# Attention scores as sums of exact float32r halves instead of float32 products

## The chip, the cores and the metric

One core of a Trainium2 chip runs the kernel. The metric is the device time of one execution in microseconds; the median of three runs is given with the lowest and the highest.

## What is computed

The reference is a chain of four blocks on x, 8 sequences of 512 tokens with 256 features, in float32:

```python
x = x + attn_a(layernorm(x))     # 16 heads of 16, softmax over all 512 keys, biases
x = x + ffn(layernorm(x))        # soft decision tree: 255 gates, 256 leaves
x = x + attn_b(layernorm(x))     # 16 heads of 16, rotary q and k, causal softmax
x = x + ffn(layernorm(x))        # the same tree again
# in both attentions, per sequence and head:
scores = q @ k.T / sqrt(16); out = softmax(scores) @ v
```

The change touches only how q, k, the row maxima of the scores and the products q @ k.T are held and computed.

## The kernel before

A "batch" n runs from 0 to 15: n below 8 is attention a on sequence n followed by the tree, n from 8 on is the causal attention b on sequence n - 8 followed by the tree. All x tiles stay on chip. The 16 heads of a batch are four groups g of four heads j. The four heads of a group lie on partitions 32j to 32j+15 of the q and k tiles, so that their products use four different groups of 32 rows of TensorE. Row 32j+16 of k holds ones (L181), and the same row of q receives minus the maximum of each query's scores, so that one product of 17 rows gives scores less maximum.

The scores are computed twice. The first time (`maxima`, L322, tiles mx) with queries on partitions, so that VectorE reduces each row to its maximum (L348; with the mask, L343, in causal batches). When a group's four query blocks are done, `put` (L352) transposes the maxima (lessT), ScalarE negates them into `rows`, and four DMAs (L360) write them to row 32j+16 of q. The second time (`scores`, L364, tiles st) with keys on partitions; ScalarE takes the exponential into pt (L381), in causal batches GpSimd zeroes the diagonal block (L523), and `weigh` (L383) multiplies with v into av (four heads on four column groups; a column of ones in v gives the sum). `divide` (L401) transposes and normalises.

The main loop (L499) has 32 steps a batch: 4 groups, 4 key blocks kt, 2 pairs of heads. In each step it issues two st products, two mx products of the batch's position 12 steps further on (LEAD, L56), the exponentials and reduces of these four tiles, every second step one `weigh`, and then one piece of other work of kind "pe" and one of kind "v" (`Units`, L63). Other work is written as generators: `pre(n)` (L260: layer norm, transpose, q, k, v), `post` (L425: output projection) and `tree` (L438). `pre(n+1)` is started 12 steps before the first st product of batch n (L509). Causal products are cut to the keys needed: widths of 512, 384, 256 and 128 columns.

PSUM has seven rotating banks (L161) that all these tiles share in order of allocation, and one for av. Each st or mx tile takes one bank until ScalarE or VectorE has read it. Engines run their instructions in order; the order on each is fixed when the program is built, where a scheduler may move an instruction that it expects to wait behind others.

`pre` makes q and k in a layout with feature rows in 128 partitions and moves them into place with DMAs on SP's queue. For n below 8 that is two DMAs of 128 KB for each of four projections' halves (L294). For causal n, ScalarE copies the projection to `eo` (L287), GpSimd computes the rotation in six operations (L302 to L306), and 16 DMAs of 64 KB (L310, eight partitions each at the destination) place q and k. q has two buffers, k two (L179), so the next batch's q is written once the batch before the current one is through.

Of the kernel before, what the change touches and what calls it, by code (L numbers as in the profile page):

```python
# [30 lines left out]

F32 = mybir.dt.float32
AF = mybir.ActivationFunctionType
ALU = mybir.AluOpType
AX = mybir.AxisListType
# [2 lines left out]
P = 128  # L41
# [14 lines left out]
LEAD = 12  # L56
# [45 lines left out]
def hybrid_kernel(ctx, tc, x, a_qk, a_v, a_o, a_qk_b, a_v_b, a_o_b, b_q, b_k, b_v, b_o,  # L102
# [24 lines left out]
    def load_x(b):  # L127
# [5 lines left out]
    make_identity(nc, ident)  # L133
    neg_half = const.tile([P, NT], F32, tag="neg_half", name="neg_half")
    nc.gpsimd.memset(neg_half, -0.5)

    load_x(0)
    wa, wb = Consts(), Consts()
    qk = load(a_qk, "a_qk")
    wa.q, wa.k = qk[:, :, :D], qk[:, :, D:]  # L140
    wa.qk_b = load_as_is(a_qk_b, "a_qk_b")
    wa.v = load(a_v, "a_v")
    load_x(1)
    wa.o = load(a_o, "a_o")
    v_b = load_as_is(a_v_b, "a_v_b")
    out_b = load_row(a_o_b, "a_o_b")

# [7 lines left out]

    raws = [
        load(w, n, pool1, tag)
        for w, n, tag in ((f_q, "f_q", "outT"), (f_routers, "f_routers", "th"),
                          (f_values, "f_values", "lp"), (f_out, "f_out", "lpT"))
    ]  # L160
    banks = ctx.enter_context(tc.tile_pool(name="banks", bufs=7, space=PSUM))  # L161
    ps_av = ctx.enter_context(tc.tile_pool(name="ps_av", bufs=1, space=PSUM))
# [1 line left out]
    def bank(shape, name):  # L164
        return banks.tile(shape, F32, tag="ps", name=name)
# [3 lines left out]
    leaf_scale = load_as_is(leaf_scale, "leaf_scale")  # L169
    for b in range(3, B):  # L170
        load_x(b)
    wb.q, wb.k, wb.v, wb.o = (load(a, n) for a, n in ((b_q, "b_q"), (b_k, "b_k"), (b_v, "b_v"), (b_o, "b_o")))
    cos = load(cos, "cos")[:, 0, :]
    sin = load(sin, "sin")[:, 0, :]


    ks, vs, qs, outs, avs, lesses = [], [], {}, {}, {}, {}
    for i in range(2):
        k = pool1.tile([P, NG, S], F32, tag=f"k{i}", name=f"k{i}")  # L179
        v = pool1.tile([P, NT, H, 2 * HD], F32, tag=f"v{i}", name=f"v{i}")  # L180
        nc.gpsimd.memset(k, 1.0)  # L181
        nc.vector.memset(v, 1.0)
        ks.append(k)
        vs.append(v)

    units = Units()
# [61 lines left out]
    def by_tokens(srcT, w, n, tt, name):  # L248
# [8 lines left out]
                )  # L257
        return ps

    def pre(n):  # L260

        causal, b = divmod(n, B)
        w = wb if causal else wa
        got = []
        yield from layer_norm(b, f"n{n}", got)
        xn = got[0]
        xnT = pool2.tile([P, NC, S], F32, tag="xnT", name=f"xnT{n}")
        qs[n] = pool2.tile([P, NG, S], F32, tag="q", name=f"q{n}")
        for c in range(NC):
            yield "pe", 0 if c else 3  # L270
            transposed(xnT, xn, c, f"xt{n}_{c}")
        for which in range(2):

            dst = (qs[n], ks[n % 2])[which]
            wt = (w.q, w.k)[which]
            if causal:
                eo = pool1.tile([P, 2, S], F32, tag="eo", name=f"eo{n}{which}")
            for c in range(NC):
                yield "pe", 0
                ps = bank([P, S], f"qk{n}{which}{c}")  # L280
                for k in range(NC):
                    nc.tensor.matmul(  # L282
                        ps, lhsT=wt[:, k, c * P : (c + 1) * P], rhs=xnT[:, k, :],
                        start=k == 0, stop=k == NC - 1,
                    )
                if causal:
                    nc.scalar.copy(eo[:, c, :], ps)  # L287
                    continue
                r = pool2.tile([P, S], F32, tag="qk", name=f"r{n}{which}{c}")
                at = 2 * which + c  # L290
                nc.scalar.activation(r, ps, AF.Identity, bias=w.qk_b[:, at : at + 1])
                for j2 in range(2):
                    j = 2 * c + j2
                    nc.sync.dma_start(dst[32 * j : 32 * j + HD, :, :], r[64 * j2 : 64 * j2 + 64, :])  # L294
            if causal:

                yield "v", 0
                by_cos = pool1.tile([P, 2, S], F32, tag="by_cos", name=f"by_cos{n}{which}")
                by_sin = pool1.tile([P, 2, S], F32, tag="by_sin", name=f"by_sin{n}{which}")
                r = pool1.tile([P, 2, S], F32, tag="rot", name=f"rot{n}{which}")  # L300
                for c in range(2):
                    nc.gpsimd.tensor_tensor(by_cos[:, c, :], eo[:, c, :], cos, ALU.mult)  # L302
                    nc.gpsimd.tensor_tensor(by_sin[:, c, :], eo[:, c, :], sin, ALU.mult)
                    yield "v", 0
                nc.gpsimd.tensor_tensor(r[:, 0, :], by_cos[:, 0, :], by_sin[:, 1, :], ALU.subtract)
                nc.gpsimd.tensor_tensor(r[:, 1, :], by_sin[:, 0, :], by_cos[:, 1, :], ALU.add)  # L306
                for c in range(2):
                    for j in range(NJ):
                        at = 32 * j + 8 * c
                        nc.sync.dma_start(dst[at : at + 8, :, :], r[32 * j : 32 * j + 32, c, :])  # L310
        for tt in range(NT // 2):
            yield "pe", 0
            ps = by_tokens(xnT, w.v, D, tt, f"v{n}{tt}")
            for i in range(2):
                to = vs[n % 2][:, 2 * tt + i, :, 0:HD]
                nc.scalar.copy(to, ps[:, i, :].rearrange("p (h d) -> p h d", h=H))
        if n == 0:
            fold_bias()
        if not causal:
            add_bias(b, out_b)  # L320

    def maxima(n, g, u, pair):  # L322

        causal = n >= B
        qt = 3 - (u + LEAD // 2) % NT
        if (u, pair) == (0, 1):
            lesses[n, g] = pool2.tile([P, NJ, NT], F32, tag="less", name=f"less{n}_{g}")
        less = lesses[n, g]
        width = (qt + 1) * P if causal else S
        got = []  # L330
        for j in (2 * pair, 2 * pair + 1):
            rows = slice(32 * j, 32 * j + HD)
            ps = bank([P, S], f"mx{n}_{g}_{qt}_{j}")
            nc.tensor.matmul(  # L334
                ps[:, :width], lhsT=qs[n][rows, g, qt * P : (qt + 1) * P],
                rhs=ks[n % 2][rows, g, :width], start=True, stop=True,
            )
            got.append((j, ps))
        for j, ps in got:
            at = less[:, j, qt : qt + 1]  # L340
            if causal:
                seen = pool2.tile([P, S], F32, tag="seen", name=f"seen{n}_{g}_{qt}_{j}")
                nc.vector.tensor_tensor_reduce(  # L343
                    out=seen[:, :width], in0=ps[:, :width], in1=mask[:, S - width :], scale=1.0,
                    scalar=LOWEST, op0=ALU.add, op1=ALU.max, accum_out=at,
                )
            else:
                nc.vector.tensor_reduce(at, ps, AX.X, ALU.max)  # L348
        if (u, pair) == (NT - 1, 0):
            units.add(put(n, g, lesses.pop((n, g))), "pe", 1, urgent=True)  # L350

    def put(n, g, less):  # L352

        ps = bank([NJ * NT, P], f"lessT{n}_{g}")
        nc.tensor.transpose(ps, less.rearrange("p j t -> p (j t)"), ident)
        rows = pool2.tile([NJ * NT, P], F32, tag="rows", name=f"rows{n}_{g}")
        nc.scalar.mul(rows, ps, -1.0)
        for j in range(NJ):
            at = 32 * j + HD
            nc.sync.dma_start(qs[n][at : at + 1, g, :], rows[NT * j : NT * (j + 1), :])  # L360
        return
        yield

    def scores(n, g, kt, pair):  # L364

        first = kt * P if n >= B else 0
        got = []
        for j in (2 * pair, 2 * pair + 1):
            ps = bank([P, S], f"st{n}_{g}_{kt}_{j}")
            rows = slice(32 * j, 32 * j + HD + 1)  # L370
            nc.tensor.matmul(  # L371
                ps[:, : S - first], lhsT=ks[n % 2][rows, g, kt * P : (kt + 1) * P],
                rhs=qs[n][rows, g, first:], start=True, stop=True,
            )
            got.append((j, ps))
        return got

    def exponentials(n, kt, got, pt):
        width = S - kt * P if n >= B else S
# [45 lines left out]
    def post(n):  # L425

        causal, b = divmod(n, B)
        outT = pool1.tile([P, NC, S], F32, tag="outT", name=f"outT{n}")
        out = outs.pop(n)
        for c in range(NC):  # L430
            transposed(outT, out, c, f"outTp{n}_{c}")
# [6 lines left out]
    def tree(n, b):  # L438
# [20 lines left out]
        for level in range(DEPTH):  # L459
# [12 lines left out]
                        pairs[:, :, :, side], of_level, one, lp, ALU.add, ALU.mult  # L472
                    )
            lp = new
        lpT = pool1.tile([P, NC, S], F32, tag="lpT", name=f"lpT{n}")
        for c in range(NC):
            yield "pe", 0 if c else 1
            transposed(lpT, lp, c, f"lt{n}_{c}")
# [20 lines left out]
    for i in range(-LEAD, total + 2):  # L499
        ahead = i + LEAD  # L500
        if ahead < total:
            n, g, u, pair = place(ahead, 1)
            if ahead % STEPS == 0:
                if n in pres:
                    units.finish(pres.pop(n))
                if 0 < n < 2 * B - 1:
                    if n + 1 >= B:
                        units.finish(trees[n + 1 - B])
                    pres[n + 1] = units.add(pre(n + 1))  # L509
        got = None  # L510
        if 0 <= i < total:
            sn, sg, kt, sp = place(i, 0)
            if sp == 0:
                pt = pool3.tile([P, NJ, S], F32, tag="pt", name=f"pt{sn}_{sg}_{kt}")
            got = scores(sn, sg, kt, sp)
        if ahead < total:
            maxima(n, g, u, pair)
        if got is not None:
            exponentials(sn, kt, got, pt)
            if sp == 1:  # L520
                if sn >= B:

# [71 lines left out]
```

## Time and profile before

| what | us |
|---|---|
| median of 3 runs (lowest to highest) | 1599.61 (1596.56 to 1602.42) |
| the profiled execution | 1595.46 |
| its span (first to last instruction) | 1593.7 |
| TensorE busy | 1481.2 |
| VectorE busy | 757.5 |
| ScalarE busy | 665.9 |
| GpSimd busy | 453.8 |
| mean granted TensorE clock | 0.862 |

Busy is the time in which at least one instruction of the engine runs. A row of the page's groups gives the line, the engine, the operation, output<-inputs, the shape and count, then the busy time and the mean duration of one in ns, then the idle time before it and what ended it. st and mx products overlap in time, so their busy times may not be added. A float32 product appears as two records, each with its own weight load (engine PEld). First st products of the batches start at 79.96 (n=0), 154.3, 245.1, 342.7, 441.1, 531.5, 633.0, 732.8, 824.1 (n=8, the first causal one), 921.8, 1011.3, 1106.0, 1195.6, 1290.3, 1379.9 and 1470.6. The page's other large groups:

```profile
L381 ACT ACTIVATE pt<-st 128x512 f32<-128x512 f32 (+3 forms) x1024 | 473.7, 517 | 488.1 <-PE mx L334 413.8
L348 DVE TENSOR_REDUCE less<-mx 128x1 f32<-128x512 f32 x512 | 328.5, 684 | 301.0 <-PE mx L334 300.3
L390 PE MATMUL av<-pt,v 128*32 128x512 f32 (+3 forms) x2048 | 272.3, 608 | 27.9 <-POOL pt L523 27.8
```

The exponential and the reduce both spend most of their idle time waiting for TensorE.

### The profile page before, as it was taken

Reading aid. Unit: us, or ns where it says so; the run is one execution under the profiler, and the core shown is the slowest. Engines: PE = TensorE matmul, PEld = TensorE weight load, DVE = VectorE, ACT = ScalarE, POOL = GpSimd, SP = SyncE. Lnnn points to the kernel's source line nnn. Section 1 sums busy time; section 2 is a strip of 40 time slices with the busy share of each in tenths; the row PEclk is TensorE's granted clock in tenths of the full one; section 3 lists DMA queues with packets and bytes.
Section 4 is the critical chain, followed back from the end, with each engine's and each line's share of the span. In section 5 each row is a group of like instructions: output and inputs, shape, how many; then the busy total and the mean of one; then the engine's idle time right before and its main releaser. Section 6 shows DMA issues by size and latency. Waiting matters only on the chain.

```text
span 1593.7 us, 22833 instructions
## 1 busy us (share of the span) xinstructions
PE 1481.2 (93%) x8276; PEld 668.1 (42%) x8276; DVE 757.5 (48%) x2247; ACT 665.9 (42%) x1443; POOL 453.8 (28%) x452
## 2 busy tenths in 40 slices
PE   4999999999999999999998898989889798989895
PEld 2333444334344434433444444445445343445444
DVE  2355655546546555455544343544444344544422
ACT  1155545445445444545454342534334343433331
POOL 7000300402104040032416245451624445251312
PEclk9599999889799988979999596977979787986767
DMA  7001001000010100100101000000101001010000
GB/s 230 17 11 18 11 1 27 2 17 12 2 27 1 28 1 1 28 1 8 22 1 28 1 14 15 23 19 14 28 1 32 10 23 19 15 28 2 14 14 13
DMA packets 24847, 31.09 MB, mean 20 GB/s; under 512 B 4000, under 2 KB 16032, under 8 KB 24736
## 3 DMA queue, kind: packets, MB, share of 16 engines
q1 hardware_dynamic: 24736, 29.64, 7.9%
q8 instruction: 66, 1.08, 0.3%
q14 instruction: 45, 0.37, 0.1%
HBM read 8.13 MB, written 4.19 MB: 8 GB/s over the span
## 4 chain that ended last, share of the span: by engine, by line
PE 84%; POOL 7%; DVE 6%; issue 1%; ACT 1%; DMA 1%; SPq 0%; POOLq 0%; DVEq 0%; ACTq 0%
PE st L371 26%; PE av L390 15%; PE mx L334 10%; PE qk L282 8%; PE z L254 5%; PE ty L254 4%; PE v L254 4%; PE y L254 4%; DVE lp L471 3%; POOL xnt L233 2%; POOL xnn L233 2%; PE oT L407 2%; PE txt L245 2%; PE lt L245 2%; PE outTp L245 1%
## 5 line engine op out<-in xcount | busy, mean ns | idle before, releaser
L381 ACT ACTIVATE pt<-st 128x512 f32<-128x512 f32 (+3 forms) x1024 | 473.7, 517 | 488.1 <-PE mx L334 413.8
L334 PE MATMUL mx<-k,q 16*128 16x512 f32 (+3 forms) x2048 | 623.5, 631 | 6.1 <-issue 6.1
L371 PE MATMUL st<-q,k 17*128 17x512 f32 (+3 forms) x2048 | 565.2, 619 | 33.4 <-DMA q<-rows 29.6
L348 DVE TENSOR_REDUCE less<-mx 128x1 f32<-128x512 f32 x512 | 328.5, 684 | 301.0 <-PE mx L334 300.3
L343 DVE CUSTOM_DVE_ANT_0 seen<-mx,mask 128x512 f32<-128x512 f32 (+3 forms) x512 | 230.7, 487 | 340.5 <-PE mx L334 331.2
L390 PE MATMUL av<-pt,v 128*32 128x512 f32 (+3 forms) x2048 | 272.3, 608 | 27.9 <-POOL pt L523 27.8
L371 PEld LDWEIGHTS st<-q,k 17*128 17x128 f32 x2048 | 183.6, 208 | 232.9 <-issue 152.2
L334 PEld LDWEIGHTS mx<-k,q 16*128 16x128 f32 x2048 | 219.5, 209 | 58.5 <-ACT pt L381 28.5
L523 POOL TENSOR_SCALAR_AFFINE_SELECT pt<-pt 128x512 f32<-128x512 f32 x128 | 81.6, 640 | 431.8 <-ACT pt L381 431.1
L229 POOL TENSOR_SCALAR ln_rstdt<-ln_mvt 128x4 f32<-128x4 f32 x16 | 3.7, 232 | 592.9 <-DVE ln_mvt L225 592.9
L390 PEld LDWEIGHTS av<-pt,v 128*32 128x32 f32 x2048 | 43.0, 115 | 199.8 <-issue 139.5
L254 PE MATMUL z<-wg,txnT 128*128 128x255 f32 x256 | 79.7, 466 | 0.5 <-ACT txnT L246 0.5
L233 POOL TENSOR_SCALAR xnt<-x,ln_mvt,ln_rstdt 128x256 f32<-128x256 f32 x64 | 77.4, 1221 | 0.3
L233 POOL TENSOR_SCALAR xnn<-x,ln_mvn,ln_rstdn 128x256 f32<-128x256 f32 x64 | 77.4, 1220 | 0.1
L254 PE MATMUL ty<-wl,lpT 128*128 128x256 f32 x256 | 73.1, 436 | 0.0
L254 PEld LDWEIGHTS z<-wg,txnT 128*128 128x128 f32 x256 | 57.2, 235 | 35.6 <-issue 10.9
L282 PE MATMUL qk<-xnT,a_qk 128*128 128x512 f32 x128 | 68.0, 661 | 0.0
L254 PEld LDWEIGHTS ty<-wl,lpT 128*128 128x128 f32 x256 | 52.5, 216 | 32.0 <-DVE x L423 8.3
L471 DVE SCALAR_TENSOR_TENSOR lp<-th,lp 128x8 f32<-128x8 f32 (+6 forms) x224 | 64.0, 322 | 3.3
L302 POOL TENSOR_TENSOR by_cos<-eo,cos 128x512 f32<-128x512 f32 x32 | 40.7, 1270 | 80.4 <-ACT eo L287 80.4
L407 PE MATMUL oT<-ident,o 128*128 128x128 f32 x256 | 47.2, 313 | 10.6 <-DVE less L343 7.8
L407 PEld LDWEIGHTS oT<-ident,o 128*128 128x128 f32 x256 | 30.4, 155 | 58.6 <-ACT pt L381 20.9
(74 smaller groups left out, 1143.8 us busy)
## 6 DMA issues: line engine op xcount, KB each, us to landing
x<-x SPq DMA_DIRECT2D x8, 512.0 KB
q<-r SPq DMA_DIRECT2D x32, 128.0 KB
k<-r SPq DMA_DIRECT2D x32, 128.0 KB
q<-rows SPq DMA_DIRECT2D x256, 2.0 KB
q<-rot SPq DMA_DIRECT2D x64, 64.0 KB
k<-rot SPq DMA_DIRECT2D x64, 64.0 KB
out<-x SPq DMA_DIRECT2D x8, 512.0 KB
a_qk<-a_qk SPq DMA_DIRECT2D x1, 512.0 KB
```

Source lines behind the costliest of these rows:

```text
L233: nc.gpsimd.tensor_scalar(xn[:, t, :], x[:, t, :], mv[:, t, 0:1], rstd[:, t : t + 1], ALU.subtract, ALU.mult)
L254: nc.tensor.matmul(ps[:, i, :n], lhsT=srcT[:, c, t * P : (t + 1) * P], rhs=w[:, c, :], start=c == 0, stop=c == NC - 1,)
L282: nc.tensor.matmul(ps, lhsT=wt[:, k, c * P : (c + 1) * P], rhs=xnT[:, k, :], start=k == 0, stop=k == NC - 1,)
L334: nc.tensor.matmul(ps[:, :width], lhsT=qs[n][rows, g, qt * P : (qt + 1) * P], rhs=ks[n % 2][rows, g, :width], start=True, stop=True,)
L343: nc.vector.tensor_tensor_reduce(out=seen[:, :width], in0=ps[:, :width], in1=mask[:, S - width :], scale=1.0, scalar=LOWEST, op0=ALU.add, ...
L348: nc.vector.tensor_reduce(at, ps, AX.X, ALU.max)
L371: nc.tensor.matmul(ps[:, : S - first], lhsT=ks[n % 2][rows, g, kt * P : (kt + 1) * P], rhs=qs[n][rows, g, first:], start=True, stop=True,)
L381: nc.scalar.activation(pt[:, j, :width], ps[:, :width], AF.Exp, scale=SCALE)
L390: nc.tensor.matmul(av[32 * j : 32 * j + 32, first:], lhsT=vs[n % 2][:, kt, g * NJ + j, :], rhs=pt[:, j, : S - first], start=kt == 0, stop= ...
L407: nc.tensor.transpose(ps[:, t, :, :].rearrange("p j d -> p (j d)"), o4[:, t * P : (t + 1) * P], ident)
L471: nc.vector.scalar_tensor_tensor(pairs[:, :, :, side], of_level, one, lp, ALU.add, ALU.mult)
L523: nc.gpsimd.affine_select(out=pt[:, :, :P], in_=pt[:, :, :P], pattern=[[0, NJ], [1, P]], compare_op=ALU.is_ge, fill=0.0, base=0, channel_m ...
```

## The change

float32r is a 32-bit format with fewer mantissa bits; a tile of that type holds rounded values. q and k are each kept as hi, the rounded value, and lo, the rest (`halves`). k holds hi on rows 32j to 32j+15 and lo on the next 16; q is kept twice, once as hi and lo and once as lo and hi. Two passes over 32 rows, one with each q tile, then add up hi*hi + lo*lo + lo*hi + hi*lo. The negated maxima are kept as two halves too, in tiles m of their own (two rows per head), and a third pass with a stationary tile of ones adds them to st. `products` replaces the products of `maxima` and `scores`: it takes the banks of all four products of a step and issues first pass by first pass, then the second passes, then the third.

```diff
+    def halves(raw, which, n, at, js, height):
+        hl = pool2.tile([P, 2, S], F32R, tag="hl", name=f"hl{n}{which}{at}")
+        nc.scalar.copy(hl[:, 0, :], raw)
+        lo_on = nc.vector if n >= B else nc.gpsimd
+        lo_on.tensor_tensor(hl[:, 1, :], raw, hl[:, 0, :].bitcast(F32), ALU.subtract)
+        hl = hl.bitcast(F32)
+        rows = height * NG
+        for i, j in enumerate(js):
+            src = hl[rows * i : rows * (i + 1)]
+            for half in range(2):
+                to = 32 * j + HD * half + at
+                back = 32 * j + HD * (1 - half) + at
+                if which:
+                    nc.sync.dma_start(ks[n].bitcast(F32)[to : to + height], src[:, half, :])
+                else:
+                    nc.sync.dma_start(qs[n][0].bitcast(F32)[to : to + height], src[:, half, :])
+                    nc.sync.dma_start(qs[n][1].bitcast(F32)[back : back + height], src[:, half, :])
...
-                for j2 in range(2):
-                    j = 2 * c + j2
-                    nc.sync.dma_start(dst[32 * j : 32 * j + HD, :, :], r[64 * j2 : 64 * j2 + 64, :])
+                halves(r, which, n, 0, (2 * c, 2 * c + 1), HD)
...
-                for c in range(2):
-                    for j in range(NJ):
-                        at = 32 * j + 8 * c
-                        nc.sync.dma_start(dst[at : at + 8, :, :], r[32 * j : 32 * j + 32, c, :])
+                    halves(r, which, n, 8 * c, range(NJ), 8)
...
+    def products(st, mx):
+        todo, got = [], ([], [])
+        if st is not None:
+            n, g, kt, pair = st
+            first = kt * P if n >= B else 0
+            for j in (2 * pair, 2 * pair + 1):
+                ps = bank([P, S], f"st{n}_{g}_{kt}_{j}")
+                rows = slice(32 * j, 32 * j + 32)
+                lhsT = ks[n][rows, g, kt * P : (kt + 1) * P]
+                two = slice(32 * j, 32 * j + 2)
+                todo.append((ps[:, : S - first], [(lhsT, q[rows, g, first:]) for q in qs[n]]
+                             + [(ones[two, :], ms[n, g][two, first:])]))
+                got[0].append((j, ps))
...
+        for i in range(3):
+            for ps, passes in todo:
+                if i < len(passes):
+                    nc.tensor.matmul(ps, lhsT=passes[i][0], rhs=passes[i][1], start=i == 0,
+                                     stop=i == len(passes) - 1)
+        return got
...
-        nc.scalar.mul(rows, ps, -1.0)
+        nc.scalar.mul(rows[:, 0, :], ps, -1.0)
+        nc.vector.scalar_tensor_tensor(
+            rows[:, 1, :], ps, -1.0, rows[:, 0, :].bitcast(F32), ALU.mult, ALU.subtract
+        )
+        ms[n, g] = pool2.tile([P, S], F32R, tag="m", name=f"m{n}_{g}")
         for j in range(NJ):
-            at = 32 * j + HD
-            nc.sync.dma_start(qs[n][at : at + 1, g, :], rows[NT * j : NT * (j + 1), :])
+            for half in range(2):
+                at = 32 * j + half
+                nc.sync.dma_start(
+                    ms[n, g].bitcast(F32)[at : at + 1, :],
+                    rows.bitcast(F32)[NT * j : NT * (j + 1), half, :],
+                )
```

The mx products have two passes (both q tiles as stationary operand, k moving). A batch's copies thus go from 8 DMAs of 128 KB to 24 (n below 8), and from 16 of 64 KB to 48 (causal n), those of the maxima from 16 to 32. The rotation of causal batches still takes six GpSimd operations, now half by half into a tile with one buffer. To make room on chip, outT and lpT share one buffer, the masked scores (seen) and the biased q and k (r) have one buffer instead of two, and the weights of attention b are loaded into the buffers of attention a's, at the start of `pre(8)` and `post(8)` instead of at the start of the kernel.

## Prediction

> **What bounds the kernel now.** First the page's busy shares, the clock row and its costliest groups.
>
> ```profile
> PE 1481.2 (93%) x8276; PEld 668.1 (42%) x8276; DVE 757.5 (48%) x2247; ACT 665.9 (42%) x1443; POOL 453.8 (28%) x452
> ...
>
> ...
> L334 PE MATMUL mx<-k,q 16*128 16x512 f32 (+3 forms) x2048 | 623.5, 631 | 6.1 <-issue 6.1
> L371 PE MATMUL st<-q,k 17*128 17x512 f32 (+3 forms) x2048 | 565.2, 619 | 33.4 <-DMA q<-rows 29.6
> ```
>
> TensorE has work 93% of the span, no other engine half of it. The change is aimed at the two groups shown. Each has 2048 records for 1024 products: a float32 product is two records. How a step of two st and two mx products runs is in the timeline of PE and PEld:
>
> ```profile
> 404.54 0.19 PEld L371 LDWEIGHTS st<-q,k 17*128 17x128 f32 x2 [0.17 <-issue]
> 404.54 0.70 PE L371 MATMUL st<-q,k 17*128 17x512 f32 x2
> ...
> 404.64 0.19 PEld L371 LDWEIGHTS st<-q,k 17*128 17x128 f32 x2
> ...
> 405.07 0.59 PE L371 MATMUL st<-q,k 17*128 17x512 f32 x2
> 405.09 0.59 PE L334 MATMUL mx<-k,q 16*128 16x512 f32 x2
> 405.61 0.19 PEld L254 LDWEIGHTS z<-wg,txnT 128*128 128x128 f32 x1 [0.76 <-issue]
> ```
>
> Four heads lie on four groups of 32 rows and run at once. 1.07 us pass from 404.54 to the next operation: 0.107 for the first weight load (second load at 404.64), 2 x 0.427 for the records (second record at 405.07 = 0.107 + 0.427), 0.11 of change-over. When mx waits for a bank that ACT still empties, the step splits (400.83 to 402.95: 2.12 us). Summed from record to record, the first half spends 1.46 us a step on st and mx.
>
> Last, the second half. Batch n=12 begins at 1195.56; SP's queue and PE's timeline near its third group (the first fence is SP, the second PE, the third windows):
>
> ```profile
> 1212.11 0.72 SPq L310 DMA_DIRECT2D q<-rot  x1
> 1212.88 2.45 SPq L360 DMA_DIRECT2D q<-rows  x4
> 1215.44 5.00 SPq L310 DMA_DIRECT2D q<-rot  x7
> 1229.35 1.86 SPq L360 DMA_DIRECT2D q<-rows  x3
> 1232.00 5.77 SPq L310 DMA_DIRECT2D k<-rot  x8
> 1237.81 0.62 SPq L360 DMA_DIRECT2D q<-rows  x1
> ```
> ```profile
> 1237.86 0.42 PE L390 MATMUL av<-pt,v 128*32 128x128 f32 x8
> 1242.62 1.19 PE L371 MATMUL st<-q,k 17*128 17x512 f32 x1 [4.34 <-DMA q<-rows]
> ```
> ```profile
> 1195.56:1242.60 47.04, 42.70 (x285) 21.16 (x285) 22.76 (x92) 19.98 (x50) 25.33 (x27) 0.99 0.18 35
> 1242.60:1266.00 23.40, 19.86 (x98) 9.60 (x99) 6.58 (x30) 5.85 (x16) 11.36 (x11) 0.50 0.00 1
> ```
>
> Copies of the next batch's k sit ahead of one maxima row; PE stands 4.34 us, and the granted clock is then 0.50 for 23.4 us. The waits view has this seven times (29.6 us in all), once a causal batch. So SP's order is a second bound, close behind TensorE.
>
> **The products.** [...] The trace has no float32r. A float32 record of 512 columns takes 0.427 us, 0.83 ns a column. [...]
>
> Banks: all four first passes now precede any second pass, so st waits for mx's banks too. [...] I take 0.30 a step (first half), 0.28 (second): 32 steps give 9.6 and 9.0 us a batch at best. [...]
>
> **The halves.** Per batch ACT adds four copies of 0.59 (row: eo L287); the residue is four POOL operations of 1.27 (row: by_cos) or, causal, four of 0.69 on DVE (row: x L423). RoPE keeps six POOL operations. With ACT at 42% and DVE at 48% this lies beside TensorE (38, 22 and 41 us over the run). The added maxima residue is some 0.25 us, 64 times, also beside. Batch 0 has no cover: three to four residues and 24 copies before the first mx, about +10, equal to its gain. The shared buffers (outT with lpT, single r, single seen) wait on work that ends steps earlier: zero, at most 1 us a batch. The weights loaded late fall in a layer norm: zero to 3 us once.
>
> **The copies.** This decides. Causal batches go from 16 to 48 copies of 64 KB (q twice, hi and lo); maxima rows from 4 to 8. In the changed program's order SP has eight rows of group 1, then 32 q and 16 k copies, then the eight rows of group 2. PE can run that group's first two passes and two more steps' passes, then all seven banks are full: the ones pass waits, and behind it everything else on PE.
>
> Supply, from the batch start: first copy +16.5 (1212.11); eight rows of 0.62 ahead, +21.5; 48 copies. The eight k copies issue in 5.77 us (0.72 each), and their packets run from 1233.3 to 1241.6 (1.03 each). Ends: 34.6 and 49.4 us; I take 0.88, between them, since the next copy's issue overlaps packets still running: 42, to +63.7. Two rows 1.2, landing and release 3: +68. Demand: PE now gets there at +42.7 (1238.3), less 18 steps x 0.28 = +37.8. It stands 30 us instead of 4.3 and resumes at +68 instead of +47.06: +21. The 14 steps left save 3.9. Net +17 a causal batch (ends +9.5 and +24.5). The 23 us at clock 0.50 follow the stop in both. [...]
>
> First half: 24 copies of 128 KB at about 0.6 are some 15 us and mostly fit. For batches 1 and 2, though, the last k residue is queued on POOL behind the next tree's normalisation (eight of 1.22, two of 2.35), and group 1's rows behind that copy: a stop of 0 to 30 us, I take 20, plus 5 for the clock, less 9.6: +15 each. Batches 3 to 6 gain 9.6 each. Batch 7 carries causal copies: stop 20, less 9.6: +10. Batch 15 has no copies after it: -9.
>
> Sum: 7 x 17 = 119; +10; -9; 2 x 15 = 30; -38; batch 0 nil: **+112**. On the profiled execution (1595.46 us, span 1593.7, 1.8 around it) that is 1707; the median of the three runs is 4 us higher, so **1710**.
>
> **Rivals.** (A) 0.56: as above; 1640 to 1790 by the copy's two ends and the POOL stop's.
> (B) 0.17: passes are port-bound (0.427), or the row groups do not overlap. [...]
> (C) 0.14: faster. The copies stream faster than the rows of before show, because successive ones now go to q's two tiles and other partitions. If 48 take 0.5 us each (24), rows land at +50 with demand at +38: PE resumes 3 later than now and the 14 steps save 4. With no POOL stop in batches 1 and 2 the sum is -7, -10, -9 and 6 x -9.6: 1515. The causal batch breaks even near 0.52 us a copy, the kernel near 0.72 without the POOL stops and near 0.6 with them (each 0.1 is 4.8 us in eight batches). Against: issue alone takes 0.72.
> (D) 0.13: passes bring nothing, since st's wait for mx's banks eats the gain, and the stops stand: 7 x 21 + 20 + 2 x 25 + 10 = 227: 1825.
>
> **Numbers.** Likeliest 1710. Below 1600 lies most of C (0.11), above 1940 half of B (0.08): range 1600 to 1940. Differences within 0.3% (about what this measurement can tell from none) need copies as fast as their issue and no POOL stops: 0.03. Faster 0.13, slower 0.84.
>
> **What would show it.** Right: st's wait for the DMA of rows, 29.6 us before, is 150 to 300; gaps of 20 to 30 us once a causal batch, at the ones pass with SP's 48 copies just ahead; the clock at 0.50 behind each; passes 0.22 apart; TensorE's share below 80%. Wrong: passes 0.43 apart (B); causal stops under 8 us (C); full steps above 1.0 us with the passes at 0.22 (D).

## The result and the profile after

The changed kernel takes 1882.36 us (median of four runs, 1871.78 to 1898.37) against 1601.01 (1596.56 to 1624.03) for the kernel before: a ratio of 1.178, 95% interval 1.167 to 1.189, or 281 us more. The forecast was 1710, 110 us more: right in sign, far too small. The profiled execution took 1871.78 us with a span of 1870.1. Some executions of a kernel get a lower clock than its others (run 5: 0.781 against 0.795 to 0.800); times leave them out, but the profiles of runs 5, 16 and 17 come from such ones, so that stretches of run 5 are not used, and those of runs 16 and 17 only side by side.

The page of the changed kernel, busy shares, the costliest groups of the products, and the DMA queue:

```profile
PE 1474.5 (79%) x9300; PEld 736.7 (39%) x9300; DVE 823.0 (44%) x2344; ACT 696.9 (37%) x1507; POOL 497.4 (27%) x482
...
L372 PE MATMUL mx<-k,q 32*128 32x512 f32 (+3 forms) x2048 | 472.4, 461 | 116.6 <-DVE less L388 48.2
...
L372 PE MATMUL st<-q,k 32*128 32x512 f32 (+3 forms) x2048 | 447.3, 467 | 23.0 <-DVE out L452 13.5
...
L372 PE MATMUL st<-m,ones 2*128 2x512 f32 (+3 forms) x1024 | 245.4, 431 | 171.6 <-DMA m<-rows 171.6
```

TensorE is hardly less busy than before (1481.2), though each of its passes is shorter, and its idle time has a new owner: the ones pass (the third pass of st), waiting 171.6 us for the maxima rows. The mean clock is 0.791 (before 0.862), that is 782 us at 0.50 instead of 441.

A step with nothing in its way, in the timeline of PE:

```profile
546.90 0.51 PE L372 MATMUL st<-q,k 32*128 32x512 f32 x2
546.91 0.50 PE L372 MATMUL mx<-k,q 32*128 32x512 f32 x2
547.24 0.39 PE L372 MATMUL st<-q,k 32*128 32x512 f32 x1
...
547.47 0.41 PE L372 MATMUL st<-m,ones 2*128 2x512 f32 x2
547.80 0.48 PE L256 MATMUL y<-a_o,outT 128*128 128x256 f32 x1
```

All four heads begin at once, the second passes follow 0.34 later (weight load and pass), the ones passes 0.23 after them, the next operation 0.33 after that: 0.90 us from 546.90 to 547.80, before 1.07. So the passes run as the change intends. The loss is elsewhere.

Where it lies, summed from the first st product of each batch in the two traces (us):

| stretch | before | after | difference | forecast |
|---|---|---|---|---|
| start and batch 0 | 154.3 | 161.5 | +7.2 | 0 |
| batches 1, 2 | 188.5 | 237.8 | +49.3 | +30 |
| batches 3 to 6 | 390.1 | 455.1 | +65.0 | -38 |
| batch 7 | 91.3 | 126.0 | +34.7 | +10 |
| batches 8 to 14 (causal) | 646.6 | 780.2 | +133.6 | +119 |
| batch 15 and the end | 123.1 | 109.5 | -13.6 | -9 |

Of the 164 us that the forecast lacks, 103 are in batches 3 to 6. There PE has no stop above 2 us. In batch 4 (begun at 496.1) it looks like this, at the starts of its second and third groups; first PE, then SP, then PE again:

```profile
526.72 0.73 PE L372 MATMUL st<-q,k 32*128 32x512 f32 x4 [0.34 <-ACT r L318]
527.68 0.73 PE L372 MATMUL mx<-k,q 32*128 32x512 f32 x2 [0.23 <-ACT outT L248]
529.19 0.73 PE L372 MATMUL mx<-k,q 32*128 32x512 f32 x2 [0.78 <-DVE less L393]
530.70 0.66 PE L446 MATMUL oT<-ident,o 128*128 128x128 f32 x4 [0.78 <-DVE less L393]
531.28 1.22 PE L372 MATMUL st<-m,ones 2*128 2x512 f32 x2
```
```profile
542.55 5.11 SPq L410 DMA_DIRECT2D m<-rows  x8
```
```profile
561.25 1.08 PE L446 MATMUL oT<-ident,o 128*128 128x128 f32 x4 [0.87 <-DVE less L393]
563.24 0.76 PE L372 MATMUL st<-q,k 32*128 32x512 f32 x1 [0.90 <-DVE out L452]
563.36 0.76 PE L372 MATMUL st<-m,ones 2*128 2x512 f32 x1
```

PE crawls: it goes on every 1.5 to 2 us, mostly when VectorE has emptied one bank. The other banks are held by st tiles that have had their first two passes and not their third. In the third group the rows had been issued by 547.7 (second fence), but the ones pass runs at 563.36: PE's instruction order, fixed when the program is built, has it there. The same tiles had their first and second passes here:

```profile
551.62 0.50 PE L372 MATMUL st<-q,k 32*128 32x512 f32 x2
...
553.28 0.50 PE L372 MATMUL st<-q,k 32*128 32x512 f32 x2
```

Counted in the order in which PE's records begin, this ones pass is 37 records behind its tile's first pass. In a step with nothing in its way it is 8 behind. One or two group starts in each batch from 0 to 14 are like this, with 35 to 54 records. The clock is then at 0.50 (555 to 586), as it was for 23.4 us after the 4.34 us stop in batch 12 of the kernel before. In batches 1 to 6 PE is idle for 87 us (before 3), and the clock is at 0.50 for 276 us (before 96). At half speed the extra 180 us lose some 90. That, with 84 us more of idle time, less the passes' gain (43 us by run 18, 58 by the forecast), comes near the 114 us that the six batches lose (an estimate). Not every late pass costs: batch 3 has one such group start and takes 96.8 us (before 98.4), while batches 4 to 6, with two each, take 119.4 each (before 97.2 on average).

In a causal batch the forecast stop is there. Batch 12 (begun at 1426.4), SP, then PE, then windows:

```profile
1443.95 0.70 SPq L278 DMA_DIRECT2D q<-hl  x1
...
1477.48 15.89 SPq L276 DMA_DIRECT2D k<-hl  x16
1493.47 17.64 SPq L410 DMA_DIRECT2D m<-rows  x16
```
```profile
1481.65 0.98 PE L372 MATMUL st<-q,k 32*128 32x384 f32 x2 [0.90 <-DVE out L452]
1499.18 1.08 PE L372 MATMUL st<-m,ones 2*128 2x512 f32 x2 [16.55 <-DMA m<-rows]
```
```profile
1444.00:1478.00 34.00, 24.82 (x207) 14.38 (x206) 18.31 (x72) 11.87 (x32) 19.49 (x22) 0.93 0.49 63
1478.00:1499.00 21.00, 2.98 (x8) 1.62 (x8) 2.98 (x6) 0.62 (x1) 7.15 (x5) 0.50 0.33 51
```

The 32 q copies move at 63 GB/s (last column), 64 KB in 1.05 us; then come 16 k copies, then the rows. PE resumes 72.8 us into the batch (forecast 68) and has stood 16.55 us (forecast 30), because it came to the stop late, at +56.2 instead of +37.8: it had waited some 12 us on the way, for VectorE and ScalarE to empty banks and for GpSimd's masks of pt.

### The profile page after: what moved, and what is told of

The parts are those of the page before. It is cut to its first block, busy times and chain, and to the rows that moved or that the text cites. A ratio compares the mean times of both kernels' runs of the same rounds, so it can differ in the third digit from the quotient of the medians.

```text
span 1870.1 us, 26343 instructions
## 1 busy us (share of the span) xinstructions
PE 1474.5 (79%) x9300; PEld 736.7 (39%) x9300; DVE 823.0 (44%) x2344; ACT 696.9 (37%) x1507; POOL 497.4 (27%) x482
## 4 chain that ended last, share of the span: by engine, by line
PE 61%; DVE 11%; POOL 8%; DMA 6%; SPq 6%; issue 4%; ACT 3%; DVEq 0%; ACTq 0%; POOLq 0%
PE st L372 15%; PE av L429 14%; PE mx L372 8%; PE qk L309 5%; SPq L276 5%; PE z L256 4%; PE ty L256 3%; DMA m<-rows 3%; PE y L256 3%; DVE less L393 3%; DVE lp L512 2%; PE v L256 2%; POOL xnt L235 2%; DMA q<-hl 2%; ACT pt L420 2%
## 5 line engine op out<-in xcount | busy, mean ns | idle before, releaser
L372 PE MATMUL mx<-k,q 32*128 32x512 f32 (+3 forms) x2048 | 472.4, 461 | 116.6 <-DVE less L388 48.2
L372 PE MATMUL st<-q,k 32*128 32x512 f32 (+3 forms) x2048 | 447.3, 467 | 23.0 <-DVE out L452 13.5
L372 PE MATMUL st<-m,ones 2*128 2x512 f32 (+3 forms) x1024 | 245.4, 431 | 171.6 <-DMA m<-rows 171.6
L429 PE MATMUL av<-pt,v 128*32 128x512 f32 (+3 forms) x2048 | 325.1, 639 | 36.5 <-POOL pt L564 35.7
L372 PEld LDWEIGHTS mx<-k,q 32*128 32x128 f32 x2048 | 225.5, 212 | 209.2 <-DVE less L388 64.8
L372 PEld LDWEIGHTS st<-q,k 32*128 32x128 f32 x2048 | 205.8, 209 | 233.6 <-issue 134.4
L372 PEld LDWEIGHTS st<-m,ones 2*128 2x128 f32 x1024 | 130.0, 224 | 200.3 <-DMA m<-rows 177.7
L267 POOL TENSOR_TENSOR hl<-r,hl 128x512 fp32r<-128x512 f32 x32 | 40.7, 1272 | 511.1 <-ACT hl L265 426.2
L309 PE MATMUL qk<-xnT,b_qk 128*128 128x512 f32 x128 | 72.0, 690 | 0.0
L327 POOL TENSOR_TENSOR by<-eo,cos 128x512 f32<-128x512 f32 x32 | 44.4, 1389 | 79.3 <-ACT eo L314 79.3
```

The source lines that it names most:

```text
L267: lo_on.tensor_tensor(hl[:, 1, :], raw, hl[:, 0, :].bitcast(F32), ALU.subtract)
L309: nc.tensor.matmul(ps, lhsT=wt[:, k, c * P : (c + 1) * P], rhs=xnT[:, k, :], start=k == 0, stop=k == NC - 1,)
L327: nc.gpsimd.tensor_tensor(part, eo[:, i, :], table, ALU.mult)
L372: nc.tensor.matmul(ps, lhsT=passes[i][0], rhs=passes[i][1], start=i == 0, stop=i == len(passes) - 1)
L429: nc.tensor.matmul(av[32 * j : 32 * j + 32, first:], lhsT=vs[n % 2][:, kt, g * NJ + j, :], rhs=pt[:, j, : S - first], start=kt == 0, stop= ...
```

## The experiments

Theories: M, late ones passes; B, the four products of a step tied to each other's banks; C, the copies; T, the passes themselves. Eighteen kernels were run, those of a group on one chip with the kernel before (runs 17 and 18 on a chip of their own). The kernel before took 1591 to 1601 us there, so a difference in us between groups is good to about 10. Stretches are from one profile of each kernel. Where only hi halves are copied, or a pass is left out, the expectation says so.

**Runs 1 to 4: the rows, the order, the ones pass, the number of copies.**

Run 1: `nc.sync.dma_start` becomes `nc.scalar.dma_start` for m.

> The changed kernel with one edit: the DMAs of the maxima rows (m<-rows) start from ScalarE's queue instead of SP's, behind no copies. Theory M (the ones pass comes late: the rows stand behind the copies of q and k on SP, and in PE's order the ones pass is put some 33 to 39 matmuls behind its group's first pass, so that open st banks fill PSUM and PE crawls or stops, and the clock goes to 0.50): the stops of 16 to 19 us (171.6 us in all) and the crawling group starts go, full steps keep their 0.90 us, so the time falls below the kernel before: 1480 to 1580 us, time at clock 0.50 from 784 us to some 450. Theory B (the four products of a step are tied to each other's banks): only the 171.6 us of DMA waits go, 1700 to 1750, crawling stays. Theory C (the transfer load itself, 65 MB, delays the rows on any queue): above 1800.

1895.83 us, ratio 1.185 (1.175 to 1.196): nothing gained, though nearly every ones pass was back in place in PE's order. The trace names two reasons. ScalarE stands while it issues:

```profile
1456.38 5.40 ACTq L410 DMA_DIRECT2D m<-rows  x8
1461.83 0.66 ACT L420 ACTIVATE pt<-st 128x256 f32<-128x256 f32 x2 [5.48 <-DMA q<-hl]
```

At that spacing, 0.675 us each, 512 issues take some 346 us of ScalarE ahead of exponentials (an estimate). And mx of the next batch waits for its k copies instead (140.0 us, 16 times): the wait moved from the rows to the last copy. The cure was worse than its queue; run 8 repeats it without ScalarE.

Run 2: in `products`, all passes of st, then all of mx.

```diff
-        for i in range(3):
-            for ps, passes in todo:
+        for part in (todo[: len(got[0])], todo[len(got[0]) :]):
+            for i in range(3):
+                for ps, passes in part:
```

> The changed kernel with the passes issued kind by kind: all three of the two st products, then both of the two mx products, so st does not wait for mx's banks; rows' DMAs stay on SP. Theory M: nothing gained, since the ones pass is as late as before (33 to 39 matmuls); full steps get longer (two row groups at a time instead of four, 0.90 to about 1.2 us): 1880 to 1980 us. Theory B: the crawl goes, 1700 to 1780.

1850.36, ratio 1.159 (1.148 to 1.169), some 32 us below the changed kernel: faster than M expected (1880 or more) and slower than B did (1780 at most). The tie between banks costs a little; it is not the loss.

Run 3: no ones pass (`[(lhsT, q[rows, g, first:]) for q in qs[n]]` is all that st gets).

> The changed kernel without the ones pass: the maxima are computed, transposed and copied to m as before but not added to the scores, so st has two passes and waits for no row. Theory M: the time falls like that of the first run, and a little further by the third pass (0.22 us in full steps): 1450 to 1560 us. Theory B: about 0.1 to 0.2 us a step less and the DMA waits gone, 1650 to 1720. If the copies of q and k themselves come too late for their batch: first passes wait for them, above 1700.

1653.15, ratio 1.035 (1.027 to 1.042). Batches 1 to 6 take 561.3 us (before 578.5, changed 692.8), so in batches 1 to 6 all the loss hangs on the ones pass. The causal ones still take 729.4 (before 646.6): there mx waits for k copies (107.7 us in the whole run).

Run 4: `qs[n]` is one tile twice; the copies to the second are left out.

> The changed kernel with one q tile instead of two (both passes read the first one, so the cross products of hi and lo are left out and the others counted twice): 16 copies a batch instead of 24, 32 instead of 48 in causal ones. PE's order keeps its late ones passes. Theory M, with copies at about 1 us each: the causal stops of 16.4 us shrink to about 3 and those of 18 us in batches 1, 2 and 7 to about 10, while the crawl of group starts stays: 1740 to 1800 us. If copies were no cause: 1870 to 1890. If the copies were all of it: below 1650.

1699.71, ratio 1.065 (1.056 to 1.073): 182 us for a third of the copies, more than expected. Batches 1 to 6 take 608.3, causal ones 708.5.

**Runs 5 to 8: passes alone, copies alone.**

Run 5: `range(1)` for the halves' copies, rows `32 * j` to `32 * j + HD`, one q tile.

> Passes without the added copies: the changed kernel, all arithmetic of the halves and all passes kept (three for st, two for mx), but only the hi halves of q and k are copied and multiplied (16 rows a pass instead of 32; the lo parts are left out of the scores), so a batch has 8 and a causal batch 16 copies as in the kernel before; the maxima keep their 8 rows. Theory C (what the change loses is the copies; the passes themselves gain about the 0.18 us a step that full steps show): 1600 less some 90 is 1510, range 1470 to 1560. Theory T (passes in lock step over four banks, and the clock that their waits bring down, lose by themselves): 1650 or more.

1615.97, ratio 1.015 (1.011 to 1.018), between the two theories. Run 7 has the same passes; its profile gives batches 1 to 6 564.7, causal 672.6, 625 us at clock 0.50.

Run 6: two more copies after each, into a spare tile.

```diff
                     nc.sync.dma_start(dst[32 * j : 32 * j + HD, :, :], r[64 * j2 : 64 * j2 + 64, :])
+                    for at in (0, 16):
+                        nc.sync.dma_start(spare[32 * j + at : 32 * j + at + HD, :, :], r[64 * j2 : 64 * j2 + 64, :])
```

> Copies without the passes: the kernel before with float32 products, and each copy of q and k followed by two more of the same size into a spare tile that nobody reads, so 24 and 48 copies a batch (to make room, outT and lpT share a buffer as in the change). Theory C: slower by most of the change's loss, since SP's queue and the transfers are as full as in the change, though a step of 1.07 us covers a little more and no halves stand in the chain: 1780 to 1950 us. Theory T: 1600 to 1650.

1915.53, ratio 1.207 (1.200 to 1.214). Copies alone cost more than the whole change, but all in causal batches: 894.9 us for seven of them (before 646.6), and 591.5 for batches 1 to 6 (before 578.5). PE in batch 12:

```profile
1473.82 1.91 PE L376 MATMUL st<-q,k 17*128 17x512 f32 x2
1510.53 1.19 PE L376 MATMUL st<-q,k 17*128 17x512 f32 x1 [34.80 <-DMA q<-rows]
```

The stop is about twice the 16.5 us of the change; why was not tried. In batches 1 to 6 the same number of copies costs 13 us here and 114 in the change. A float32 st product has its row among its operands: it is not begun before the row is there, and leaves no bank half filled.

Run 7: run 5's copies in three pieces each.

> The fifth run's kernel with each copy of a hi half cut into three DMAs along the tokens (as many DMAs as in the change, as few bytes as in the kernel before). If the number of DMAs on SP's queue is what costs (0.67 to 0.72 us each to issue): 150 to 250 us above the fifth run. If the bytes are (128 KB in 1.06 us back to back): within 40 us of it.

1614.47, ratio 1.015 (1.008 to 1.022): as run 5. With the bytes of the kernel before, the number of DMAs costs nothing.

Run 8: `nc.gpsimd.dma_start` for m.

> The changed kernel with the maxima rows' DMAs on GpSimd's queue, since on ScalarE's queue each of them took 0.675 us of ScalarE's own time (346 us in all) ahead of the exponentials. PE's order again has every ones pass 8 matmuls behind its first pass. Theory C: the wait moves on to the copies of k, as in the run without the ones pass (1653 us, where 107.7 us of mx's waits are for k's copies), plus a third pass of some 0.2 us a step: 1700 to 1790. If rows behind the copies were the whole cause: below 1600. If GpSimd's issues are as dear as ScalarE's were, and delay its masking of pt: above 1850.

1798.47, ratio 1.131 (1.127 to 1.135), the upper end of what C expected. Every ones pass is back in its place, and batches 1 to 6 fall to 594.4. The causal ones do not (822.9): the mx products wait 128.6 us for k copies, and GpSimd issues 512 DMAs.

Passes alone +1.5% and copies alone +20.7% looked like an answer. They are not: in batches 1 to 6 neither loses what both together lose.

**Runs 9 to 12: opened tiles, two streams, lighter and heavier steps.**

Run 9:

```diff
-                todo.append((ps[:, : S - first], [(lhsT, q[rows, g, first:]) for q in qs[n]]
-                             + [(ones[two, :], ms[n, g][two, first:])]))
+                todo.append((ps[:, : S - first], [(ones[two, :], ms[n, g][two, first:])]
+                             + [(lhsT, q[rows, g, first:]) for q in qs[n]]))
```

> The changed kernel with the ones pass as the first of st's three passes, so that a score tile is not begun before its maxima rows have landed and no half-finished tile holds a PSUM bank; copies, queues and pass counts stay. Theory O (in batches 1 to 7 the copies cost so much because late ones passes leave opened banks; the copies alone added only some 2 us a batch there in the sixth run): batches 1 to 6 fall from 115 us to about 100, causal ones stay near 111: 1750 to 1810. Rival (the rows' lateness itself, whatever PE does meanwhile): 1850 to 1890.

1726.01, ratio 1.083 (1.076 to 1.091): 156 us for the order of three passes, more than expected. Batches 1 to 6 take 557.1 us, 136 less than in the change and 21 less than in the kernel before; causal ones 781.3, as in the change. Windows over batches 1 to 6 in the kernel before, the changed kernel and this one (length, busy time of PE, PEld, DVE, ACT and POOL, clock, DMA share, GB/s):

```profile
154.29:732.80 578.51, 575.74 (x3077) 235.38 (x3077) 315.01 (x646) 281.28 (x538) 97.98 (x83) 0.92 0.05 12
161.53:854.38 692.85, 605.67 (x3462) 273.20 (x3462) 322.62 (x670) 290.13 (x560) 126.20 (x105) 0.80 0.21 29
156.90:714.00 557.10, 506.91 (x3464) 251.30 (x3460) 319.46 (x671) 290.98 (x560) 126.17 (x105) 0.93 0.26 36
```

Same bytes, queues and passes, yet the clock is back at 0.93: the loss of batches 1 to 6 needs tiles that are opened ahead of their rows. (The build orders PE's instructions anew, so the late pass and the open tile go together here; one without the other was not tried.)

Run 10: `nc.gpsimd.dma_start` for the copies to `qs[n][1]`.

> The changed kernel with the copies to the second q tile on GpSimd's queue instead of SP's, so two streams run side by side, which at any time write different partitions (hi rows and lo rows). If a copy's rate is set by the few partitions it writes (64 KB to 8 partitions in 1.05 us, 128 KB to 16 in 1.06 us): the 32 q copies of a causal batch take some 20 us instead of 33.6, and the causal stops of 16.4 us shrink to about 5, less what GpSimd loses on about 0.5 us an issue: 1740 to 1820. If all DMA engines together are at their limit at this rate: 1860 to 1900.

1693.33, ratio 1.060 (1.050 to 1.070), a larger gain than expected. Causal batches fall to 677.3 from 780.2. Batches 1 to 6 fall too, to 605.6 from 692.8, though PE's order still has late ones passes there: with fewer copies ahead of the rows, most of the loss goes too. It needs both, late rows and open tiles. The q copies of batch 12 run like this (windows; last column GB/s):

```profile
1301.00:1320.00 19.00, 17.31 (x141) 11.37 (x141) 12.90 (x50) 9.83 (x25) 15.35 (x24) 1.00 0.76 90
```

90 GB/s instead of 63; the last of them are through at about 1324, some 24 us after the first instead of 33. So the DMA engines were not at their limit in the change. The q copies that write 8 partitions ran at 62 GB/s in the changed kernel (64 KB in 1.05 us, batch 12), those that write 16 at 116 (16 q copies of batch 4, 128 KB in 1.13 us each). No run had two queues that write the same partitions, so the second queue and the other partitions were not told apart.

Run 11: `k` and `q` tiles of F32R in the kernel before, memset and DMAs through `bitcast(F32)`.

> The kernel before with q, k and the maxima row held as float32r and each product a single pass (the low mantissa bits are left out of the scores); copies, rows and steps as in the kernel before. Theory P (time is TensorE's columns): a full step falls from 1.07 to about 0.43 us, 0.64 x 512 = 328 us less at most: 1280 to 1400. Theory K (a lighter step leaves TensorE waiting for ScalarE, VectorE and banks, and the clock at 0.50 for longer takes back much of it): 1450 to 1570, with more than the 443 us at clock 0.50 of the kernel before.

1412.22, ratio 0.886 (0.879 to 0.892), between the two theories; the clock is 0.861, as before. Lighter products do pay when each is one instruction and brings no more copies: 183 of 328 us.

Run 12: in run 5, `for again in range(2 if i == 0 else 1)` around the first pass.

> The fifth run's kernel (copies as in the kernel before, only hi halves) with every first pass issued twice, the second overwriting the first: 0.22 us more TensorE work in each full step, nothing else. Theory P (time is TensorE's columns): 512 x 0.22 = 110 us more than the fifth run, 1700 to 1730. Theory K (the passes' gain is lost to the clock, which falls when TensorE has too little to do between waits): time at clock 0.50 falls from some 630 to 720 us towards 450 and the run stays within 30 us of the fifth, 1590 to 1650.

1840.63, ratio 1.154 (1.144 to 1.164). Both theories fail. The extra round is 0.23 us in a full step (600.02, .35, .59, .82 in the trace), yet costs 0.44, and 912 us are at clock 0.50 (625 in run 7). More work for TensorE did not raise the clock, so a want of work is not what lowers it here.

**Runs 13 to 18: do the causes add up, and the halves.**

Run 13: the edits of runs 9 and 10.

> The changed kernel with both cures: the ones pass first, and the copies to the second q tile on GpSimd's queue. If opened tiles and the single stream are two causes that add up (the one in batches 1 to 7, the other in the causal ones): the ninth run's batches 0 to 7 (829.7 us) and the tenth's from 8 on (747.4) give 1577, range 1540 to 1620. If both cures met the same cause, one of them alone being enough: 1670 to 1700.

1632.19, ratio 1.031 (1.024 to 1.038), 250 us below the changed kernel, between the two expectations. The 1577 rests on 747.4 us for run 10 from batch 8 on; its trace has 787.1, which makes 1617, close to the result. The cures don't simply add (156 and 189 us alone). Batches 1 to 6 take 542.2: the two gain 136 and 87 us there alone and 151 together, so they meet the same loss. Causal ones take 697.9, 21 more than with the second queue alone: with the ones pass first, PE stands some 11 us at it in each.

Run 14: run 5 with run 9's edit.

> The fifth run's kernel (only hi halves, copies as in the kernel before) with the ones pass first. Theory O (the passes' gain of 0.18 us a step was lost to opened tiles at the causal batches' third groups, where the ones pass is 38 matmuls behind): 1530 to 1580. If it was lost to the tie between four products or to the halves' arithmetic: 1600 to 1630.

1634.63, ratio 1.031 (1.023 to 1.040): no gain. Opened tiles are not what cost the passes alone their gain.

Run 15: run 14 with run 2's edit.

> The fourteenth run's kernel with st's passes issued before mx's, so that st does not wait for mx's banks. If the tie costs (the second run, with the same edit, was 32 us below the changed kernel): 20 to 60 us below the fourteenth run. If not: up to 60 us above it, since two row groups at a time take 0.2 us more in full steps.

1629.42, ratio 1.030 (1.022 to 1.038), within the error of run 14. Nor is it the tie.

Run 16: in the kernel before, after each r (and each half of the rotated one):

```diff
+    def halves(raw, n):
+        hl = pool1.tile([P, S], F32, tag="hl", name=f"hl{n}")
+        nc.scalar.copy(hl, raw)
+        lo_on = nc.vector if n >= B else nc.gpsimd
+        lo_on.tensor_tensor(hl, raw, hl, ALU.subtract)
```

> The kernel before with the arithmetic of the halves alone: a copy of q and k on ScalarE and a difference on GpSimd (VectorE in causal batches), whose results nobody reads; products, copies and rows as before (outT and lpT share a buffer, as in the change). If this arithmetic hides beside TensorE, as forecast: within 10 us of the kernel before. If it delays the chain to the copies or the masks of pt: 20 to 80 us slower.

1680.66, ratio 1.060 (1.050 to 1.070): the arithmetic that was to hide costs some 90 us. ScalarE in batch 12:

```profile
1297.82 0.62 ACT L263 COPY hl<-rot 128x512 f32<-128x512 f32 x1 [3.79 <-POOL rot L313]
1298.35 0.38 ACT L391 ACTIVATE pt<-st 128x256 f32<-128x256 f32 x1
```

The copy stands 3.79 us for GpSimd's rotation, and behind it, in ScalarE's order, an exponential for which PE's next bank waits. (hl has one buffer here, which may be part of the cost.)

Run 17: both halves of causal batches on GpSimd.

> The sixteenth run's kernel (the kernel before with the halves' arithmetic alone) with the causal batches' hi copy and difference both on GpSimd, right behind its rotation, so that neither ScalarE nor VectorE waits for GpSimd ahead of exponentials and maxima. If those waits are the loss: the causal batches' 10 us each go, 1595 to 1625. If the arithmetic's amount is: unchanged or worse, since GpSimd takes 1.27 us where VectorE took 0.69, 1670 to 1720.

1606.46 us in one execution, so there is no ratio; run 16's were 1667.6 to 1682.6. The profiles give causal batches 653.5 us against 711.3, and batches 1 to 6 582.6 against 578.8. GpSimd does more here, and most of the loss is gone: it was not the amount of GpSimd's work. The wait in ScalarE's order is gone, and so are ScalarE's copies and VectorE's differences themselves (by the forecast's rows 2.4 and 2.8 us a batch); the wait is the likelier cause of 8.3 us a batch, but the two were not told apart.

Run 18: the edits of runs 9, 10 and 17 in the changed kernel.

> The changed kernel with the three cures: ones pass first, copies to the second q tile on GpSimd's queue, and the causal halves made on GpSimd. If the waits for the halves cost 10 us a causal batch here too: 1632 less 50 to 80, 1550 to 1590, below the kernel before. If GpSimd, which then has rotation, halves, 16 issues of 0.55 us and the masks of pt in one queue, becomes the late one: 1640 to 1700.

1611.74, ratio 1.017 (1.009 to 1.025), 271 us below the changed kernel but not below the kernel before; neither expectation came true. Batches 1 to 6 take 535.8 us, 7.1 less each than before. Batch 7 (124.2, before 91.3) and the causal ones (676.5, before 646.6) still pay for the copies: PE stands 28.1 us at the ones pass in batch 7 and 11 to 17 us in each of batches 8 to 14, waiting for the rows.

## Why the prediction was wrong

- **The full step**: shorter, as forecast, 0.90 us against 1.07 before. Passes lie 0.23 apart (forecast 0.22), so rival B (0.427) falls. No run shows the 0.30 and 0.28 us a step on which the sum rests: a step with nothing in its way gained 0.17. The gain in a whole batch, forecast at 9.6, is 7.1 in run 18 (0.22 a step); part of that may be the clock, which was at 0.50 for 61 us in those six batches (before 96). In the change the gain was lost.
- **The copies in the first half: the step that failed.** "24 copies of 128 KB at about 0.6 are some 15 us and mostly fit", and so "Batches 3 to 6 gain 9.6 each"; they lost 65 us instead of gaining 38. Two things were wrong. The 0.6 is what SP takes to issue one copy (median 0.60 in the kernel before), where copies came two at a time (packets of a pair: 1.75 us); back to back a copy takes 1.13, so that 24 take some 26 us and rows come later. But late rows alone cost little (run 6: 13 us in six batches). What costs is that a tile is opened ahead of its row: the prediction saw for causal batches that "all seven banks are full", and put at nothing that PE's order, which could be read beforehand, has the ones pass far behind at group starts of the first half too. Run 9 gives back 136 us in batches 1 to 6 by that alone.
- **The stops in batches 1 and 2** (20 us each): 17.6 and 18.9 measured. The sum there is 19 too low, which is what the forecast gain of two batches comes to.
- **The causal batches** (+17 each): measured +19, and the waits for rows, 171.6 us in all, lie in the forecast 150 to 300. That the sum came so close is partly luck. In batch 12 PE resumed 4.8 us later than forecast (a q copy took 1.05 us, not 0.88) and gained 8.5 us instead of 3.9 on the steps after that (39.2 against 47.7). The stop itself is shorter than forecast only because PE came to it 18 us later. Copies alone do it (run 6), and a second stream undoes most of it (run 10).
- **The halves** ("beside TensorE"): wrong in causal batches. The sum of busy time was read, not who stands behind a waiting copy. Alone it costs 8.3 us a causal batch (run 16 against run 17). Within the change it seems to cost less, 3 us a causal batch between runs 13 and 18 (697.9 and 676.5 in all); that the rest is hidden under the stop is likely and not shown.
- **The banks** ("st waits for mx's banks too"): right, at a small price; run 2, without that wait, gains 32 us net, 0.06 a step.
- **Batch 7** (+10): +34.7. Its copies are causal ones. The stop was 17.8 us, forecast 20; the gain of 9.6 did not come, and the clock was at 0.50 for 58 us (before 7). What each of these costs was not separated. Run 18 still has +33, with a stop of 28.1.
- **Rivals.** D's time (1825) was the nearest, for a part of its reason: gains eaten by full banks. But what filled the banks was the ones pass behind its row, not st waiting for mx.

Open: why passes alone (runs 5, 7, 14, 15) gain nothing. Causal batches lose 26 us there (run 7), about half of what lies between runs 16 and 17 (58). In batches 1 to 6 they gain 2 to 3.5 us each, not 7. Those runs multiply 16 rows instead of 32, and have more time at clock 0.50 (below); whether the rows are the reason was not tried.

## What to carry to other kernels

When one product becomes several accumulating passes, put the pass whose operand comes last first: a tile that is begun holds its bank until its last pass. That paid where the row comes during other work (136 us in batches 1 to 6 of run 9), and cost some time where the row is late anyway (21 us in the causal batches of run 13). Cost a row of copies by what copies take back to back (here 1.13 us for 128 KB and 1.05 for 64 KB), not by what it takes to issue them (0.60 and 0.67). Try a second queue whose copies write other partitions at the same time (run 10: 90 GB/s instead of 63). "Beside the bottleneck" holds only if nothing on the engine waits in front of work that the bottleneck needs (in run 16 a copy stood 3.79 us ahead of an exponential).

## What the runs showed of the hardware

- A 2 KB packet of the copies in batches 1 to 6 took 84 ns (median) in the kernel before, where two copies at most follow each other, and 269 ns in the change, where eight or sixteen do. Copies of 128 KB ran at about 150 GB/s in a pair and at 116 in the 16 q copies of batch 4.
- A single queue's rate was not one number: the 16 k copies of batch 12, of which each writes other rows than the one ahead of it, took 14 us in the changed kernel (about 75 GB/s), the 32 q copies 33 us (63). Whether the order of the q copies in the queue would help was not tried.
- Eight DMA issues in a row took 5.40 us of ScalarE (run 1) and 4.42 us of GpSimd (run 10), 0.675 and 0.55 us each, ahead of their other work; SP took 0.57 us for a row and 0.67 for a copy of 64 KB (medians).
- Time at clock 0.50 in batches 1 to 6 was 195, 191 and 143 us in runs 7, 14 and 15 (passes over 16 rows), 82, 75 and 61 in runs 9, 13 and 18 (32 rows), and 96 in the kernel before; run 12, with more passes over 16 rows, had most of all in the whole run (912 us). The number of rows alone does not decide it: run 11, with single passes over 16 and 17 rows, had 65. What does is open.
